# A four-layer graph network: layer 2's x turned by VectorE and ScalarE instead of TensorE, under a newly recorded order of steps

## The chip, the cores and the metric

The kernel runs on one core of one Trainium2 chip. The metric is device time in microseconds (us), the median over runs; smaller is better. A core has five engines with instruction queues of their own: TensorE (PE; its weight loads are shown apart as PEld), VectorE (DVE), ScalarE (ACT), GpSimd (POOL) and SyncE (SP), which here issues transfers. Engines wait for each other by semaphores. Within one queue the instructions stay in the order in which the program lists them.

## The reference, cut to what matters

Thirty-two graphs of 512 nodes with 256 features, fp32. Each goes through four layers, each with a residual and a layernorm:

```
x = layernorm(x + relu(((1 + eps) x + adj @ x) @ W1 + b1) @ W2 + b2)          # layer 0
x = layernorm(x + graph_attention(x, adj > 0.5; W, a_src, a_dst) + bias)      # layer 1, 4 heads
q, k, v = x @ Wq.T, x @ Wk.T, x @ Wv.T                                        # layer 2, 8 heads of 32
p = softmax(q k.T / sqrt(32) + log(adj + 1e-6))
x = layernorm(x + (p @ v) @ Wo.T + bo)
s = ((x @ W) @ x.T) * adj, masked by nodemask                                 # layer 3
x = layernorm(x + softmax(s) @ x)
```

## The kernel before, in words

**Steps.** `graph(g)` describes the work of one graph as named steps. A step has an engine, a cost in us, the steps that it comes after, the buffers that it takes and frees, and a function that emits its instructions. Transfers are steps of queues (`q1` for transfers issued by SP, `qa` for accumulating ones issued by POOL). `plan.run` puts the steps of all 32 graphs (and of the preparation, graph 0 of the plan) into one order, so that several graphs are in flight at once: while one is in layer 0, another is in layer 1, and so on. In the kernel before, `Plan.order` chooses at each point among the steps that can start soon the one that is due first; the due times come from a fixed period per graph, the length of the work left behind a step, and a long table of shifts, partly apart for the first and the last graphs (`edges`). The steps' costs serve this choice alone. The emitted order is the order in each engine's queue.

**Buffers.** SBUF tiles come from numbered stocks: 13 of kind B (8 KB per partition), 12 of kind C (4 KB), 10 of D (2 KB); PSUM has eight banks p.

**One graph.** x lies as a tile of 128 partitions x 4 chunks of nodes x 256 features, with nodes on the partitions.
- Layer 0: the adjacency is loaded by four transfers (`la0` to `la3`, line 821) and turned by VectorE (line 880); h0, h1 (hT_ps), f0 to f3 (h1T_ps), y0 and y1 (y_ps) are products on TensorE; then the residual (line 695), statistics (638, 639), one power on POOL (661), and the layernorm's four pieces on ScalarE (line 684, steps r10 to r13; r20 to r23 behind layer 1, r30 to r33 behind layer 2).
- Layer 1: x is turned on TensorE (line 978), v10 to v13, R_t (line 1035), the attention weights z on ScalarE (1104) and VectorE (1115), the products o_ps (1137), the denominators (1175), y_t (1204, 1205).
- Layer 2: x is needed with features on the partitions. `features_first(2)` turns it: two steps xt20, xt21, each with four 128x128 TensorE transposes into a PSUM bank (line 1241, xT_t), each followed by a ScalarE copy of 128x512 (line 1245, steps xe20, xe21). `proj` makes q and k (steps q0, q1, k0, k1, evicted by qe and ke, line 1264), `values` makes v (v20 to v23, evicted at line 1280). Eight scores steps s0 to s7 (line 1293) with four exps each on ScalarE (line 1306) and two multiplications by the adjacency on VectorE (line 1315), eight products n0 to n7 (line 1351). The weights are summed by accumulating POOL transfers (cd steps, line 1326; fd steps, line 1379), and d2 (line 1398) makes denominators of the sums. p0, p1 (o2p_ps) are the output projection.
- Layer 3: x (as x3) is turned by `turned`: one write to DRAM, four reads in a pattern, two VectorE transposes (line 742), save for the first two and the last three graphs, which use `features_first(3)`. Then iT (i0, i1), t0 to t3, exps (1545), w0 to w3.
- The bias of the next layer is added to x by an accumulating POOL transfer (`bias_steps`, line 625); for layer 2's bias it comes after the steps xt20, xt21.

`product` writes a matrix product in one of two forms: whole (line 342, array 128x128) or, if the step before left the array in 32-column tiles, as four 32-column pieces (line 346, array 128x32). Scores use an array of 32x128, d2 one of 64x32.

`moved`, which turns x in quadrants, stands in the kernel before, but nothing calls it.

Of the kernel before, what the change touches and what calls it, by code (L numbers as in the profile page):

```python
# [16 lines left out]
P = 128  # L17
# [19 lines left out]

class Step:
# [4 lines left out]
    def __init__(self, eng, us, after, take, mode, emit):  # L43
        self.eng, self.us, self.after, self.take, self.emit = eng, us, after, take, emit
        self.mode = mode
        self.then, self.frees = [], []


class Plan:
# [51 lines left out]
    def link(self):  # L101

        self.left = [{} for _ in self.steps]
        for g in reversed(range(len(self.steps))):
            steps, left = self.steps[g], self.left[g]
            for name, s in steps.items():
                for a in s.after:
                    (self.steps[0][a[1:]] if a[0] == "^" else steps[a]).then.append((g, name))
            for k, (_, after) in enumerate(self.frees[g]):
                for a in after:  # L110
                    steps[a].frees.append(k)
        for g in reversed(range(len(self.steps))):
            steps, left = self.steps[g], self.left[g]
            for name in reversed(steps):
                s = steps[name]
                left[name] = s.us + max(
                    (self.left[h][n] + self.hop(s, self.steps[h][n]) for h, n in s.then if h - g < 2),
                    default=0.0,
                )
# [6 lines left out]
    def ready(self, g, name, ends):  # L126

        s, t = self.steps[g][name], 0.0
        for a in s.after:
            h, n = (0, a[1:]) if a[0] == "^" else (g, a)  # L130
            t = max(t, ends[h][n] + self.hop(self.steps[h][n], s))
        return t

    def order(self, period, ahead, window, stay, rush=(), moves=(), edges=(0, (), 0, (), ())):


        room = {b: [(0.0, i) for i in range(n)] for b, n in self.stock.items()}
        engine, mode, out, last = {}, "", [], 0.0
        held = [{} for _ in self.steps]
        ends = [{} for _ in self.steps]  # L140
        waits = [{n: len(s.after) for n, s in steps.items()} for steps in self.steps]
        fwaits = [[len(after) for _, after in frees] for frees in self.frees]
        ready, low, opened = {}, 0, 0
        todo = [len(steps) for steps in self.steps]
        moved = dict.fromkeys((n for steps in self.steps for n in steps), 0.0)
        turn = [max(g - 1, 0) for g in range(len(self.steps))]
        for i, early in enumerate(rush):
            turn[-1 - i] -= early
        for n, far in moves:
# [1947 lines left out]
```

## Time and profile before

| | |
|---|---|
| median of 3 runs | 2767.73 us (2764.44 to 2769.32) |
| profiled execution, its own time | 2767.12 us |
| its span, first to last instruction | 2765.3 us |
| granted TensorE clock, mean | 0.994 |
| PE busy | 2716.7 us, 28680 matmul records |
| DVE busy | 2158.8 us, 4257 instructions |
| ACT busy | 1720.4 us, 3320 instructions |
| POOL busy | 474.8 us, 526 instructions |
| DMA queue of POOL's transfers / of SP's | 53.1% / 24.2% of 16 engines |

How to read it: the profile is one execution, recorded by the hardware. "Busy" is the time in which an engine ran at least one instruction; one matrix product in fp32 makes two matmul records, and records of neighbouring instructions overlap by about 0.1 us, so the pitch from start to start is shorter than the mean duration. A row such as "out<-in ... x508 | 273.9, 593 | 179.6 <-X" gives the shapes, the count, the busy time in us, the mean duration in ns, and the idle time of the engine just before such instructions with who ended most of it. In a timeline, merged rows give start, length, engine, line, tiles and count, with an idle time in brackets where there was one. Line numbers are those of the kernel before.

### The profile page before, as it was taken

The numbers are of one execution on the slowest core, as the hardware profiler recorded it, in microseconds if no ns is written. First come the engines' busy times: TensorE is split into PE (matmuls) and PEld (weight loads), VectorE is DVE, ScalarE is ACT, GpSimd is POOL, SyncE is SP. The second block draws the span as 40 slices with busy tenths as digits, with TensorE's granted clock in tenths as the row PEclk, the third lists the DMA queues.
The fourth block names the chain that finished last, engine by engine and source line by source line (L and its number), as shares of the span: only waits on it lengthen the run. The fifth ranks groups of instructions, "written<-read, shape, count | busy, mean of one in ns | idle before, by whom it ended". The sixth has DMA issues, their size and how long they took to land.

```text
span 2765.3 us, 68089 instructions
## 1 busy us (share of the span) xinstructions
PE 2716.7 (98%) x28680; PEld 1317.9 (48%) x28680; DVE 2158.8 (78%) x4257; ACT 1720.4 (62%) x3320; POOL 474.8 (17%) x526
## 2 busy tenths in 40 slices
PE   8999999999999999999999999999999999899998
PEld 6544444444445444445444445444444443444443
DVE  3887778877879877879877879877878877578975
ACT  3676665666666666666666666666665665556853
POOL 1111211121111121111121111121111111111110
PEclk9999999999999999999999999999999999999999
DMA  8487787778888879888878888888896988736760
GB/s 167 80 168 150 148 168 147 160 160 163 158 163 151 171 157 169 162 156 153 174 162 160 149 171 151 171 157 169 155 163 135 182 168 163 156 73 146 155 131 17
DMA packets 476735, 418.76 MB, mean 151 GB/s; under 512 B 377788, under 2 KB 431496, under 8 KB 444552
## 3 DMA queue, kind: packets, MB, share of 16 engines
q0 software_dynamic: 45568, 277.89, 53.1%
q1 hardware_dynamic: 429872, 136.18, 24.2%
q8 instruction: 227, 3.72, 0.5%
q14 instruction: 84, 0.69, 0.1%
q10 hardware_dynamic: 984, 0.28, 0.0%
HBM read 155.53 MB, written 31.24 MB: 68 GB/s over the span
## 4 chain that ended last, share of the span: by engine, by line
PE 86%; DVE 6%; DMA 3%; issue 2%; ACT 1%; POOL 0%; SPq 0%; DVEq 0%; POOLq 0%; ACTq 0%
PE s L1293 8%; PE o_ps L1351 7%; PE v_ps L346 7%; PE y_ps L342 7%; PE o_ps L346 6%; PE o_ps L1137 6%; PE hT_ps L346 6%; PE s L346 5%; PE h1T_ps L346 4%; PE o2p_ps L346 3%; PE iT_ps L342 3%; PE s L342 3%; PE h1T_ps L342 3%; PE kT_ps L342 2%; DVE z L1115 2%; PE qT_ps L346 2%
## 5 line engine op out<-in xcount | busy, mean ns | idle before, releaser
L1315 DVE SCALAR_TENSOR_TENSOR z<-AT,z 128x1024 f32<-128x1024 f32 x512 | 612.6, 1214 | 108.2 <-ACT z L1306 107.0
L1306 ACT ACTIVATE z<-s 128x512 f32<-128x512 f32 x1024 | 541.4, 608 | 109.2 <-PE s L1293 103.4
L1104 ACT ACTIVATE z<-R_bc,nT,S 128x512 f32<-128x512 f32 x512 | 373.4, 807 | 72.0 <-DMA z<-z 58.2
L684 ACT ACTIVATE x<-x,shift,rstd 128x256 f32<-128x256 f32 x508 | 273.9, 593 | 179.6 <-DVE shift L669 174.8
L1115 DVE SCALAR_TENSOR_TENSOR z<-z,T,edge 128x512 f32<-128x512 f32 x512 | 346.5, 742 | 5.8 <-ACT z L1104 5.8
L1326 POOL DMA_DIRECT2D z<-z x186 | 174.4, 942 | 868.4 <-PE o_ps L1351 445.3
L661 POOL TENSOR_TENSOR rstd<-ve,nhalf 128x4 f32<-128x4 f32 (+1 forms) x131 | 169.0, 1339 | 854.8 <-DVE ve L655 846.6
L1293 PE MATMUL s<-qT,kT 32*128 32x512 f32 x2048 | 278.4, 626 | 0.4 <-ACT kT L1264 0.4
L1351 PE MATMUL o_ps<-z,v 128*32 128x512 f32 x2048 | 254.9, 599 | 2.6 <-DVE z L1315 1.4
L1539 DVE TENSOR_TENSOR z<-s,AT 128x512 f32<-128x512 f32 x128 | 88.4, 690 | 214.9 <-PE s L342 110.1
L1137 PE MATMUL o_ps<-z,v 128*32 128x512 f32 x2048 | 233.8, 595 | 2.5 <-DVE z L1115 2.5
L1165 DVE TENSOR_TENSOR z<-z 128x1024 f32<-128x1024 f32 (+1 forms) x256 | 229.5, 949 | 0.7 <-PE o_ps L1137 0.7
L638 DVE BATCH_NORM_STATS2 st<-x 128x6 f32<-128x256 f32 x508 | 212.7, 419 | 10.6
L346 PE MATMUL o_ps<-x,z 128*32 128x257 f32 x3520 | 202.4, 380 | 0.0
L346 PE MATMUL hT_ps<-AT,x 128*32 128x256 f32 (+2 forms) x2640 | 185.5, 380 | 0.0
L342 PE MATMUL y_ps<-w_sb,h1T 128*128 128x256 f32 x832 | 184.4, 379 | 0.0
L342 PEld LDWEIGHTS y_ps<-w_sb,h1T 128*128 128x128 f32 x832 | 156.1, 190 | 21.5 <-issue 1.0
L1293 PEld LDWEIGHTS s<-qT,kT 32*128 32x128 f32 x2048 | 96.7, 184 | 143.5 <-issue 63.6
L346 PEld LDWEIGHTS o_ps<-x,z 128*32 128x32 f32 x3520 | 114.8, 110 | 83.8 <-issue 6.9
L346 PE MATMUL h1T_ps<-hT,w_sb 128*32 128x512 f32 x1296 | 147.9, 595 | 0.0
L625 POOL DMA_DIRECT2D x<-biases x96 | 103.8, 1081 | 237.0 <-issue 67.7
L346 PE MATMUL s<-iT,xT 128*32 128x512 f32 x1232 | 139.4, 592 | 0.1
(188 smaller groups left out, 3858.7 us busy)
## 6 DMA issues: line engine op xcount, KB each, us to landing
z<-z POOLq DMA_DIRECT2D x186, 1024.0 KB, 8.7
x<-biases POOLq DMA_DIRECT2D x96, 512.0 KB, 9.6
R_bc<-R_dram SPq DMA_DIRECT2D x32, 1024.0 KB
Ar<-in_adj_dram SPq DMA_DIRECT2D x124, 256.0 KB
z<-z POOLq DMA_DIRECT2D x62, 512.0 KB, 7.7
x<-in_x_dram SPq DMA_DIRECT2D x32, 512.0 KB
out_dram<-x SPq DMA_DIRECT2D x31, 512.0 KB
x_dram<-x SPq DMA_DIRECT2D x27, 512.0 KB
```

The source lines that it names most:

```text
L342: nc.tensor.matmul(out, lhsT, rhs, start=start, stop=stop)
L346: nc.tensor.matmul(out[part], lhsT[:, part], rhs, start=start, stop=stop)
L638: nc.vector.bn_stats(t[f"st{n}"][:, c, :], t["xo" if n == 4 else "x"][:, c, :D])
L684: nc.scalar.activation(t[into][:, c, :D] if into else xn, xn, AF.Identity, bias=t[f"shift{n}"][:, c : c + 1], scale=t[f"rstd{n}"][:, c : c ...
L1104: nc.scalar.activation(t[f"e{h}"][:, c, :], t["Rbc"][:, h, :], AF.Relu, bias=t["nT"][:, h, c : c + 1], scale=t["S"][:, h, c : c + 1],)
L1115: nc.vector.scalar_tensor_tensor(z, z, t["T"][:, h, c : c + 1], t["edge"][:, c, :], op0=ALU.add, op1=ALU.mult)
L1137: nc.tensor.matmul(po[32 * q : 32 * q + 32, :], t["v"][:, c, hp * P + 32 * q : hp * P + 32 * q + 32], t[f"e{2*hp+q//2}"][:, c, :], start=( ...
L1165: nc.vector.tensor_add(z[:, :m, :], z[:, :m, :], z[:, m : 2 * m, :])
L1293: nc.tensor.matmul(pk, t["k"][hs, o, blk(c)], t["q"][hs, o, :], start=True, stop=True)
L1306: nc.scalar.activation(t[f"E{k}"][:, j, :], t[f"ps{k}{j}"], AF.Exp, scale=QSCALE)
L1315: nc.vector.scalar_tensor_tensor(z, t["AT"][:, c, None, :].to_broadcast([P, 2, N]), ADJ_EPS, z, op0=ALU.add, op1=ALU.mult,)
L1351: nc.tensor.matmul(t[f"n{o}"][32 * j : 32 * j + 32, :], t["v2"][:, c, o * P + F2 * j : o * P + F2 * (j + 1)], t[f"E{k}"][:, j, :], start=( ...
```

## The change

Graphs that are `near` an end (the first two and the last three) keep `features_first(2)`. The other 27 call `moved(2, ("L2",), "x", True)`: two VectorE transposes of 128x512 (steps xu20, xu21) turn each 32x32 block in place within its group of 32 partitions, into one more C buffer xU2, and sixteen ScalarE copies (four steps xe20 to xe23 of four copies) move each group's blocks to the right group of partitions. Each copy has 32 partitions and 256 elements, in runs of 32. q, k and v wait for all four steps. The bias transfer of layer 2 comes after xu20, xu21. The planned cost of such a copy step is set higher.

The search inside `Plan.order` is gone. `ORDER`, a compressed text, holds the order of all steps; `sequence` unpacks it, and `run` follows it, keeping only the books on buffers and on the array's shape. The order was found with the planner's costs, its two ends in a search of their own in which transfers stand in order of issue. It differs from the old one in every part, the middle too.

```diff
+ORDER = (
+    'c-rk;*_PwF4FmyhT5P$OxqWjd{r|riRDqP;bMl<LNZqz&i3?CzNFA1$(mW)I;A6ZAPv)V1h{k2S`xpPFqmF8{pty-!xZnlMkL3T7'
...
+)
...
-    def order(self, period, ahead, window, stay, rush=(), moves=(), edges=(0, (), 0, (), ())):
...
+    def sequence(self, text):
+        data = zlib.decompress(base64.b85decode(text))
+        left, low = [list(steps) for steps in self.steps], 0
+        for ahead, place in zip(data[: len(data) // 2], data[len(data) // 2 :]):
+            g = low + ahead
+            yield g, left[g].pop(place)
+            while low < len(left) and not left[low]:
+                low += 1
...
+        for g, name in self.sequence(text):
...
+            s.emit()
...
+        XE2 = DC if near else 4
...
-                    f"xe{n}{b}", "act" if shared else "dve", 1.35 if shared else 1.6,
+                    f"xe{n}{b}", "act" if shared else "dve", 1.66 if shared else 1.6,
...
-        features_first(2, ("L2",))
-        bias_steps(3, row("xt2", DC))
+        if near:
+            features_first(2, ("L2",))
+            bias_steps(3, row("xt2", DC))
+        else:
+            moved(2, ("L2",), "x", True)
+            bias_steps(3, row("xu2", DC))
...
-                f"{n}{o}", "pe", 1.72, row("xe2", DC) + prev(n, o) + (f"^we{n}",),
+                f"{n}{o}", "pe", 1.72, row("xe2", XE2) + prev(n, o) + (f"^we{n}",),
...
-                f"v2{c}", "pe", 0.86, row("xe2", DC) + prev("v2", c) + ("^wev",),
+                f"v2{c}", "pe", 0.86, row("xe2", XE2) + prev("v2", c) + ("^wev",),
...
+        plan.run(ORDER)
```

The body of `moved` for this call (it is unchanged, and not called before):

```
for d in range(DC):                      # steps xu2d, VectorE
    nc.vector.transpose(xU[:, d, :] as (p c f), x[:, :, blk(d)])
for b in range(4):                       # steps xe2b, ScalarE
    for a in range(4):
        nc.scalar.copy(xT[32b:32b+32] at [j, d, c, a, i], xU[32a:32a+32] at [j, d, c, b, i])
```

## The prediction

> **What bounds the kernel now.** I read the page's busy shares first, then busy time by stretches of the span, then one graph's TensorE timeline, then the waits of TensorE and the rows by shape.
>
> From the page, busy time by engine and TensorE's share in 40 slices:
> ```profile
> PE 2716.7 (98%) x28680; PEld 1317.9 (48%) x28680; DVE 2158.8 (78%) x4257; ACT 1720.4 (62%) x3320; POOL 474.8 (17%) x526
> ...
> PE   8999999999999999999999999999999999899998
> ```
> Busy time by stretches (length, then PE, PEld, DVE, ACT, POOL, clock, DMA):
> ```profile
> 600.00:900.00 300.00, 300.00 (x3335) 146.80 (x3331) 247.91 (x494) 189.72 (x362) 54.18 (x57) 1.00 0.84 158
> ...
> 2100.00:2400.00 300.00, 286.06 (x3129) 130.37 (x3122) 213.55 (x422) 170.58 (x329) 51.49 (x57) 0.98 0.83 162
> ...
> 2700.00:2766.00 66.00, 52.30 (x466) 24.69 (x458) 33.60 (x86) 22.94 (x41) 5.68 (x9) 0.92 0.05 18
> ```
> In the middle TensorE has no idle time, while ScalarE idles 37% and VectorE 17% of it. All 48.6 us of TensorE's idle time (2765.3 less 2716.7) is at the two ends: 16 us up to 600 and 33 us after 2100, by the same view.
>
> One graph's turn in the middle, in TensorE's timeline (start, length, work):
> ```profile
> 1002.27 0.28 PE L1035 MATMUL R_t<-ident,R 128*18 128x128 f32 x1
> ...
> 1054.92 3.60 PE L342 MATMUL iT_ps<-xT,w_sb 128*128 128x512 f32 x8
> 1058.35 1.04 PE L1241 MATMUL xT_t<-ident,x 128*128 128x128 f32 x8
> 1059.32 1.92 PE L1351 MATMUL o_ps<-z,v 128*32 128x512 f32 x16
> ...
> 1085.24 0.28 PE L1035 MATMUL R_t<-ident,R 128*18 128x128 f32 x1
> ```
> R_t comes once per graph, so a graph costs 82.97 us. Nothing between the two rows has an idle mark: the period is TensorE's work. The eight xT_t transposes of layer 2 hold TensorE from 1058.35 to 1059.32.
>
> A page of the Trainium skill speaks against this reading: Perfetto Trace Analysis, Identifying the Most-Contended Engine, calls matmul busy time a poor measure and goes by weight loads. By that rule (PEld 48%) VectorE at 78% would be the engine to spare, and this change, which loads it more, would bring no gain. The rows of start times decide: one matmul follows the other at a fixed pitch.
>
> **The change part by part.**
>
> *Transposes off TensorE, 27 graphs.* Of the 0.97 us above, 0.10 is the price of the next row's other array shape (one 128-column transpose follows another at 0.109 us in the timeline; the last is 0.2 before the o_ps). So 8 x 0.109 = 0.87 us, times 27 = **23.5 us off the bounding engine**. This is on the path, since no other engine fills those stretches.
>
> *Array shapes.* Each change of tiling (128x128, 128x32, 32x128, 64x32) costs TensorE 0.09 to 0.11 us: 128x512 matmuls start 0.43 apart inside a shape and 0.52 across a border. The instruction order of the two programs has 541 borders before and 474 after. Borders out of the 32x128 scores are free, for the next scores step starts 0.51 later as well; without them 354 become 303. 51 x 0.105 = **5.4 us less**, nearly all at the ends (the middle has 17 paying borders per graph in both). Many y_ps and h1T_ps products change between 128x128 and 128x32; that is free, as eight 256-column records take 1.73 us in either (x32 rows of 7.06 and of 1.93 per quarter).
>
> *Added on VectorE.* Two 128x512 transposes per graph. The nearest rows are the adjacency's and layer 3's; on ScalarE, the copies' neighbours are these (busy, mean ns, idle before):
> ```profile
> L684 ACT ACTIVATE x<-x,shift,rstd 128x256 f32<-128x256 f32 x508 | 273.9, 593 | 179.6 <-DVE shift L669 174.8 <-DVE rd_all L1565 4.7
> ...
> L1545 ACT ACTIVATE z<-z,node_off 128x512 f32<-128x512 f32 x128 | 89.8, 718 | 50.8 <-DVE z L1539 50.8
> ...
> L938 ACT ACTIVATE h1T<-h1T_ps,b_sb 128x512 f32<-128x512 f32 x128 | 87.9, 687 | 81.0 <-PE h1T_ps L346 51.8 <-PE h1T_ps L342 29.0
> ...
> L880 DVE STREAM_TRANSPOSE AT<-Ar 128x512 f32<-128x512 f32 x124 | 77.7, 678 | 0.0
> ...
> L1245 ACT COPY xT<-xT_t 128x512 f32<-128x512 f32 x74 | 42.6, 591 | 69.2 <-PE xT_t L1241 69.2
> ...
> L1280 ACT COPY v<-v_ps 128x256 f32<-128x256 f32 x128 | 41.5, 385 | 22.8 <-PE v_ps L346 17.6 <-PE v_ps L342 4.9
> ```
> 2 x 0.69 x 27 = 37 us more, 2196 of about 2730, 80%. It lies beside TensorE's work.
>
> *Added on ScalarE.* Sixteen copies of 32 partitions x 256 elements, SBUF to SBUF, from one group of 32 partitions to another. No row has that. Low end: L1280, the same element count out of PSUM, whose four take 1.20 us in the timeline, 0.27 each as they overlap. High end: a 128x512 activation from SBUF (L1104) at 807 ns, about 0.71 per piece back to back. In between lies L684 (SBUF, 256 elements, with scale and bias) at 593, four in 2.08 us, 0.49 each. SBUF instead of PSUM costs 31 ns (L1545 against L938), so a bare copy is 385 + 31 = 416 ns; I take **0.42 us** a piece, with no overlap counted, as the four-part pattern is not in the trace. 16 x 0.42 = 6.7 us; two evictions of about 0.48 go. Net 5.7 x 27 = 154 us: ScalarE at 1874, 69%.
>
> The other rule to weigh: the Trainium skill's VectorE: DVE Perf Modes, Rules for kernel authors, gives 128x128 transposes to TensorE where the result may land in PSUM. By it each graph would trade 0.87 + 1.0 us for 1.4 + 6.7 and lose 6 us, 167 in all. The stretch of 600 to 900 answers that this is true of work, but not of time: there ScalarE has 110 us idle in 300 and TensorE none.
>
> *Does the longer chain stay hidden?* q, k and v2 now wait for four copy steps. In the new order, from the end of scores step s7 TensorE does n4, y0, y1, i0, n5, n6, i1, n7 and then k0 of the waiting graph: 0.96 + 6.94 + 1.73 + 1.74 + 1.73 + 0.87 = 14.0 us by the pitches. ScalarE in that time: three exps at 0.48, four layernorm pieces at 0.49, three exps: 4.9, so free at 5.0; VectorE's two transposes (0.60 back to back) run from the last layernorm piece at 3.6 to 4.9. Copies from 5.0 to 11.8. **2.1 us to spare**; up to 0.55 us a copy is hidden. Behind the copies on ScalarE stand the evictions of i1 and i0, due later (i1 ends at 13.1). The x tile's bias DMA on POOL (L625, landing in 9.6) now waits for VectorE's transposes instead of TensorE's, and is needed by x30 more than 50 us later: nothing. The turned tile holds one more of the twelve C buffers from the transposes to the last copy, about 8 us of each turn; a later tile's first write could wait for it, which I leave within the new waits below.
>
> *The ends.* One wait there is large (TensorE timeline):
> ```profile
> 2375.25 3.74 PE L346 MATMUL v_ps<-wg_sb,xT 128*32 128x264 f32 x64
> 2386.96 3.41 PE L346 MATMUL iT_ps<-xT,w_sb 128*32 128x512 f32 x16 [7.96 <-DVE xT L742]
> ```
> iT waits 7.96 us for layer 3's x on its way through DRAM, and then runs at half pace (3.41 for sixteen records that else take 1.9): 9.5 us lost. Counted in the orders, the TensorE work between the last layernorm piece r33 and i0 of such graphs grows from 18 to 19 us to 21 to 28. I take 8 us won here. The remaining starts (4.47 us until the first adjacency, 3.3 more in the next rows) and the serial last graph stand in both orders. Bounds for the ends: all 33 us of tail idleness won, or 20 us of new waits, as one new 8 us wait like this at each end costs.
>
> Sum, against the profiled execution (2767.1 us, span 2765.3, so 1.8 around it): 2767.1 - 23.5 - 5.4 - 8.0 = 2730.2. New waits in the middle I put at 0.1 us a graph, 3 us: **2733**. The median of the runs shown, 2767.73, is 0.6 above the profiled one, within rounding of this.
>
> **The rivals.**
> *Transfers take over the middle.* The sum of the denominators d2 comes after a chain of three accumulating DMAs; in the middle the last lands only 0.4 to 3.2 us before d2 starts, and layer 3's x lands 0 to 3.4 us before its transposes. The new order leaves 24.4 us of TensorE work from n7 to d2 instead of 26.0, and 18.2 instead of 19.1 from r33 to i0. If the chains take as long as now, up to 1.2 us a graph is waited: 27 x 1.2 = 32; half of that on average gives about 2749, all of it 2762. Against: n6 to d2 is unchanged (26.9), and n6 is what the chain waits for. Chance 0.22.
> *The copies come late* (the slower side). Place: k0 waits for the sixteenth copy. The gain of 37 us is gone when the wait is 1.4 us a graph, that is at 3.5 us over the 6.7, or 0.64 a copy. At L1104's 0.71, 11.3 us, the wait is 2.5 us: 2733 + 27 x 2.5 = 2800. For: the pattern is in no row. Against: 256 elements, not 512, and no scale or bias. With other orders' mishaps, chance 0.10.
> *The change doesn't do what it says*: TensorE's saved time reappears as idle time before the same waits, the period stays 82.97. About 2765. Chance 0.04.
> *The ends gain more*: 20 us or so of the tail's idleness; 2712. Chance 0.12.
>
> **How the numbers follow.** The forecast, 2720 to 2745, has 0.52, and its time is the predicted one. The range of 2705 to 2763 takes in the better ends and the transfers' case, and leaves out about 0.05 below and 0.13 above. About 0.2% (5.5 us) is what a measurement of this kernel can tell from no change. Faster: 0.52 + 0.22 + 0.12 = 0.86; same 0.04; slower 0.10.
>
> **What would show it.** Right: R_t to R_t at about 82.1 us in the middle, with TensorE at 300 of 300; xT_t rows of L1241's kind down from 296 to 80; ScalarE near 69%, each copy near 0.42 us; no 8 us wait before iT. Wrong: an idle mark at kT_ps released by ScalarE's copy (the second rival), at d_ps or iT_ps released by a DMA or VectorE (the first), or a tail with more than 33 us idle.

## The result, and the profile after

The changed kernel takes **2796.52 us** (median of 4 runs, 2791.48 to 2805.82) against 2767.28 for the kernel before (4 runs): 1.0115 times as long, 95% interval 1.0098 to 1.0133. It is slower by 29 us where the forecast was faster by 35. The profiled execution took 2792.94 us, with a span of 2791.2.

The busy shares and TensorE's 40 slices, as they were read before:
```profile
PE 2706.1 (97%) x30576; PEld 1297.3 (46%) x30576; DVE 2185.6 (78%) x4311; ACT 1854.5 (66%) x3698; POOL 469.1 (17%) x526
...
PE   9999999999999999999999999999999999989998
```
TensorE has less work than before (2706.1 against 2716.7 us), and more idle time: 85.1 us instead of 48.6. The slices cannot show it, since a 9 stands for 90% and more. The first of the stretches shown before does (length, then PE, PEld, DVE, ACT, POOL, granted clock, DMA share, GB/s):
```profile
600.00:900.00 300.00, 284.92 (x3367) 137.57 (x3363) 234.63 (x468) 194.27 (x390) 50.32 (x55) 0.98 0.77 150
```
From 600 to 900 TensorE was busy all 300 us before; now it lacks 15 us there, and its granted clock is 0.98 instead of 1.00. The waits name the place (us in total, times, longest):
```profile
DVE xT L721 <- DMA xL<-x_dram: 62.1, 11, 10.2
...
PE iT_ps L324 <- DVE xT L721: 47.8, 10, 7.3
```
Before, the second kind of row had one wait, of 8.0 us. Now iT, layer 3's first product, waits ten times for VectorE's transposes of layer 3's x, and these wait for the reads of that x from DRAM. One wait is near the end (7.3 us), one is of 0.3 us, and eight are in the middle, 4.5 to 5.4 us each, 40.3 in all.

Two graphs of the changed kernel side by side, in TensorE's timeline (start, length, work, the idle time before it in brackets). The first one is late, the second is not:
```profile
1054.19 7.09 PE L324 MATMUL y_ps<-w_sb,h1T 128*32 128x256 f32 x128
1066.23 3.64 PE L324 MATMUL iT_ps<-xT,w_sb 128*32 128x512 f32 x16 [4.95 <-DVE xT L721]
1069.61 3.05 PE L1339 MATMUL o_ps<-z,v 128*32 128x512 f32 x16
...
1144.57 7.09 PE L324 MATMUL y_ps<-w_sb,h1T 128*32 128x256 f32 x128
1151.51 1.92 PE L324 MATMUL iT_ps<-xT,w_sb 128*32 128x512 f32 x16
1153.23 1.93 PE L1339 MATMUL o_ps<-z,v 128*32 128x512 f32 x16
```
The late graph pays twice: it waits 4.95 us, and then sixteen records take 3.38 us from start to start instead of 1.72. The granted clock (column before the last two) tells why. The two stretches lie behind the late and the timely iT:
```profile
1066.00:1071.00 5.00, 4.77 (x24) 1.35 (x28) 4.90 (x10) 0.00 (x0) 0.00 (x0) 0.50 1.29 142
...
1151.00:1156.00 5.00, 5.00 (x58) 1.86 (x52) 4.90 (x10) 4.86 (x13) 0.47 (x1) 1.00 0.83 150
```
In every trace here this clock changes only on a fixed grid, whose slots are 3.41 us long. Four slots around the late iT, in the same columns:
```profile
1061.65:1065.07 3.42, 0.00 (x0) 0.00 (x0) 0.00 (x0) 3.32 (x10) 0.00 (x0) 1.00 1.09 146
1065.07:1068.48 3.41, 2.25 (x12) 0.68 (x16) 3.11 (x4) 0.73 (x2) 0.00 (x0) 0.50 1.17 135
1068.48:1071.90 3.42, 3.42 (x20) 0.89 (x16) 3.25 (x10) 0.00 (x0) 0.00 (x0) 0.50 1.09 111
1071.90:1075.31 3.41, 3.41 (x36) 1.07 (x32) 0.98 (x6) 0.87 (x2) 1.92 (x2) 1.00 0.39 78
```
The slot in which TensorE did nothing is followed by half the clock, and the first slot that it worked through is followed by the full clock. In the eight late graphs the half clock lasts one slot (three times) or two (five times).

By the starts of R_t a timely turn takes 82.4 us and the eight late ones 88.9 to 90.7: together 59.6 us over 82.4, or 7.45 a late graph, of which 5.0 is the wait and 2.4 the slow matmuls behind it.

The span in three stretches, by the fifth and the twenty-fifth R_t:

| kernel | before the 5th R_t | 20 turns | after the 25th R_t | span |
|---|---|---|---|---|
| before | 335.8 | 1662.1 | 767.4 | 2765.3 |
| changed | 321.7 | 1694.4 | 775.1 | 2791.2 |
| x3, the changed kernel with the reads on time | 320.5 | 1649.8 | 759.3 | 2729.6 |

### The profile page after: what moved, and what is told of

Same layout as the page of the kernel before. It is cut to its first block, busy times and chain, and to the rows that moved or that the text cites. A ratio compares the mean times of both kernels' runs of the same rounds, so it can differ in the third digit from the quotient of the medians.

```text
span 2791.2 us, 72411 instructions
## 1 busy us (share of the span) xinstructions
PE 2706.1 (97%) x30576; PEld 1297.3 (46%) x30576; DVE 2185.6 (78%) x4311; ACT 1854.5 (66%) x3698; POOL 469.1 (17%) x526
## 4 chain that ended last, share of the span: by engine, by line
PE 68%; DVE 16%; DMA 8%; issue 2%; SPq 2%; ACT 2%; POOL 1%; ACTq 0%; POOLq 0%; DVEq 0%
PE s L1281 7%; DVE z L1094 6%; PE o_ps L1339 6%; PE v_ps L324 5%; PE s L324 5%; PE h1T_ps L320 5%; PE iT_ps L324 4%; PE y_ps L324 4%; DMA xL<-x_dram 4%; PE o_ps L1116 4%; DVE z L1144 3%; PE o_ps L324 3%; PE hT_ps L324 3%; PE s L320 2%; DMA x_dram<-x 2%; DVE z L1303 2%
## 5 line engine op out<-in xcount | busy, mean ns | idle before, releaser
L1303 DVE SCALAR_TENSOR_TENSOR z<-AT,z 128x1024 f32<-128x1024 f32 x512 | 604.4, 1209 | 51.8 <-ACT z L1294 51.4
L1314 POOL DMA_DIRECT2D z<-z x186 | 172.3, 929 | 979.4 <-PE o_ps L1339 348.8
L324 PE MATMUL o_ps<-x,z 128*32 128x257 f32 x3680 | 210.8, 380 | 0.0
L324 PE MATMUL hT_ps<-AT,x 128*32 128x256 f32 (+2 forms) x2736 | 193.5, 382 | 0.5 <-issue 0.4
L320 PE MATMUL h1T_ps<-hT,w_sb 128*128 128x512 f32 x424 | 191.0, 592 | 0.0
L324 PE MATMUL y_ps<-w_sb,h1T 128*32 128x256 f32 x3392 | 188.7, 379 | 0.0
L761 ACT COPY xT<-xU 32x256 f32<-32x256 f32 x432 | 173.9, 402 | 12.0 <-DVE xU L742 6.3
L917 ACT ACTIVATE h1T<-h1T_ps,b_sb 128x512 f32<-128x512 f32 x128 | 86.6, 687 | 143.2 <-PE h1T_ps L320 128.7
L324 PE MATMUL iT_ps<-xT,w_sb 128*32 128x512 f32 x992 | 131.6, 658 | 47.8 <-DVE xT L721 47.8
L324 PEld LDWEIGHTS o_ps<-x,z 128*32 128x32 f32 x3680 | 136.0, 110 | 79.4 <-issue 14.9
L324 PE MATMUL s<-iT,xT 128*32 128x512 f32 x1472 | 165.9, 592 | 0.0
```

What stands on the lines that cost most here:

```text
L320: nc.tensor.matmul(out, lhsT, rhs, start=start, stop=stop)
L324: nc.tensor.matmul(out[part], lhsT[:, part], rhs, start=start, stop=stop)
L1303: nc.vector.scalar_tensor_tensor(z, t["AT"][:, c, None, :].to_broadcast([P, 2, N]), ADJ_EPS, z, op0=ALU.add, op1=ALU.mult,)
```

## The experiments

Theory: in the new order a 1 MB adding transfer of GpSimd (step cd5, L1314) is issued at the same time as the last of the four reads of layer 3's x. A read that comes to the DMA engines behind it lands only with it. Rival 1: the new work of VectorE or ScalarE is late, not the reads. Rival 2: there are too many bytes for the stretch, in whatever order.

The queues in the late graph (start, length, queue, work), GpSimd's first, then SyncE's:
```profile
1038.39 1.20 POOL L1314 DMA_DIRECT2D z<-z  x1
1050.15 0.82 POOL L1367 DMA_DIRECT2D z<-z  x1 [10.56 <-DMA z<-z]
...
1055.46 0.94 POOL L1314 DMA_DIRECT2D z<-z  x1
```
```profile
1040.10 0.57 SPq L689 DMA_DIRECT2D x_dram<-x  x1
1051.05 5.25 SPq L702 DMA_DIRECT2D xL<-x_dram  x4
1056.46 12.05 SPq L800 DMA_DIRECT2D Ar<-in_adj_dram  x4
```
The write of x goes out at 1040.10, 1.7 us behind a first adding transfer (cd2), and has landed only when that one has, 10 us later (L1367, which waits for cd2, follows at 1050.15). So the reads start at 1051.05; the last is issued at 1055.6, just behind cd5 at 1055.46. It lands at 1065.2, and cd5 at 1064.7. Over the middle graphs of this kernel, counted from the write: cd5 is always issued at +15.3 or +15.4; last reads issued up to +14.9 land at about +18 to +20, in time for iT at +21; those issued at +15.2 and later land at +25; at +15.0 both occur. (The issue of a read takes 0.6 us or more on SyncE's queue; by its end the border is sharp: in time up to +15.70, late from +15.71.)

Why a read lands with the adding transfer is in the packets of the two queues, which the trace counts, each with its size (packets, MB, share of 16 engines; q0 is GpSimd's queue, q1 SyncE's). First the 3 us from 1059 of the late graph, while cd5 is on its way, then the 1 us from 1064, when its packets are through:
```profile
DMA packets 146, 0.61 MB, mean 202 GB/s; under 512 B 73, under 2 KB 73, under 8 KB 73
q0 software_dynamic: 73, 0.60, 103.1%
q1 hardware_dynamic: 73, 0.01, 4.1%
```
```profile
q1 hardware_dynamic: 1214, 0.15, 147.1%
```
The read consists of 1024 packets of 128 bytes, cd5 of 128 packets of 8 KB. While both queues have work, the packets go one for one: 73 to 73 here, 24 of SyncE's in a microsecond instead of 1214. So what is left of a read when cd5's packets start (1.5 to 2.6 us behind its issue) is still mostly there when they end. In the midst of cd5, 87 of its packets went with 32 to 145 of SyncE's in the twenty middle graphs, median 85.5. The write of x, packets of 1 KB, is held by cd2 in the same way (92 to 95 from 1043 to 1047).

| run | us (median) | against before, 95% |
|---|---|---|
| x1 add later | 2733.81 | 0.9885 (0.9869 to 0.9902) |
| x2 load before read | 2898.68 | 1.0484 (1.0462 to 1.0507) |
| x3 write first | 2730.48 | 0.9872 (0.9855 to 0.9888) |
| x4 turns doubled, on x1 | 2759.76 | 0.9982 (0.9973 to 0.9992) |
| x5 sums first, on x3 | 2735.76 | 0.9885 (0.9857 to 0.9913) |
| x6 both moves of x1 and x2 | 2788.41 | 1.0081 (1.0054 to 1.0108) |
| x7 half the copies doubled, on x3 | 2808.34 | 1.0153 (1.0131 to 1.0175) |
| x8 turn in the planner's own new order | 3645.29 | 1.3179 (1.3153 to 1.3205) |
| x9 order alone | 2882.24 | 1.0427 (1.0409 to 1.0444) |
| x10 order alone, write first | 2877.66 | 1.0417 (1.0395 to 1.0439) |
| x11 three edits on the changed kernel | 2727.95 | 0.9866 (0.9850 to 0.9883) |
| x12 turn alone in the old order | 2937.44 | 1.0621 (1.0599 to 1.0642) |
| x13 add in two, on x2 | 2876.54 | 1.0403 (1.0373 to 1.0433) |
| x14 add in four, on x2 | 2869.48 | 1.0378 (1.0348 to 1.0408) |
| x15 add behind the reads, on x2 | 2755.83 | 0.9977 (0.9947 to 1.0006) |

The edits move steps in the fixed order: `run` makes a list of what `sequence` yields, changes it, and follows it. The expectations below count nine late graphs in the middle; one of these was the wait of 0.3 us, so it is eight.

### x1: the second adding transfer later
```diff
+        for g in range(4, 27):
+            order.remove((g, "n4"))
+            order.insert(order.index((g + 2, "y0")) + 1, (g, "n4"))
```


> The changed kernel, with one step moved in its fixed order: the product of z and v of one head (step n4, o_ps at L1339, 8 matmuls, 1.06 us) goes behind the first half of the next graph's y_ps product (3.5 us of TensorE), which delays the 1 MB adding transfer behind it (L1314, cd5) by about 3 us. Theory (order of issue): in 9 of the 22 middle graphs of the changed kernel the last of the four reads of layer 3's x (L702) was issued beside or behind that transfer, 15.0 to 15.6 us after the write, and landed only with it, at +25; iT then waited 5 us and ran slowly behind, 7.5 us a graph. With the transfer issued at about +18 every read goes first: no iT wait in the middle, turns of 82.4 us, 2796 - 9 x 7.5 = 2729 us (2720 to 2740). Rival 1 (the vector transposes and scalar copies of the new turn are late, not the reads): nothing of them is moved, 2796 us. Rival 2 (the transfers are too many bytes for the stretch whatever their order): the wait moves to the d2 product, which the later transfer feeds, 2785 to 2800 us.

Measured: 2733.81 us. In the middle cd5 goes out at +18.3 to +18.9, and last reads issued as late as +16.1 land at +20.8 or sooner. The waits (us in total, times, longest):
```profile
PE iT_ps L328 <- DVE xT L725: 5.9, 5, 4.2
```
4.2 of the 5.9 us is the wait near the end; the middle has 1.7. No work of VectorE or ScalarE was moved, so rival 1 falls; no byte was taken away, and d2 does not wait, so rival 2 falls.

### x2: the last read later
```diff
+        for g in range(5, 26):
+            order.remove((g + 4, "la0i"))
+            order.insert(order.index((g, "xl33i")), (g + 4, "la0i"))
```


> The changed kernel, with the issue of one load of a later graph's adjacency (la0, Ar at L800) moved ahead of the last of the four reads of layer 3's x on the same issuing engine, in 21 middle graphs: the last read is issued some 0.7 to 1.2 us later, nothing else is moved. Theory (order of issue): nearly all those reads are now issued behind the 1 MB adding transfer that goes out at +15.3 and land with it, so that 18 to 21 graphs wait in place of 9: 9 to 12 more x 7.5 = 2864 to 2886 us. Rival 1 (vector and scalar work late): the same time, 2796 us. Rival 2 (bytes, not order): the bytes are the same, within 1 us a graph, 2796 to 2810 us.

Measured: 2898.68 us, a little over the expected range. All 21 graphs wait:
```profile
PE iT_ps L328 <- DVE xT L725: 127.4, 21, 12.1
```
One of the 21 is the long wait near the end; a wait of 4.6 us of the middle is put down to a ScalarE copy and stands in another row. By graph, the 21 of the middle wait 119.8 us, 5.7 each, and their turns are 89 to 92 us. The bytes are the same as in the changed kernel. But this load also puts its own 256 KB ahead of the read; x6 and x15 take that apart.

### x3: the write first
```diff
+                if k == 2 and 5 <= g <= 25:
+                    nc.gpsimd.tensor_copy(little([P, 1], "hold2"), graphs[g - 1]["x3"][:, 3, :1])
                 nc.gpsimd.dma_start(dst, src, accum_op=ALU.add)
```


> The changed kernel, with a copy of 128 x 1 elements on GpSimd ahead of the first 1 MB adding transfer (L1314, cd2), which reads the last quarter of layer 3's x: the transfer is so issued just behind the write of that x to DRAM (L689) in place of 1.7 us ahead of it. Theory (order of issue): the write then lands some 4 to 5 us after its issue and not at +8 to +10 with the transfer, the reads go out at +5 to +9 and land before the second transfer is issued at +15.3; no iT wait, 2796 - 68 = 2729 us (2720 to 2745), if the later first transfer does not make the d2 product late (it landed 1.8 to 6.3 us ahead of it). Rival 1: 2796 us. Rival 2: the d2 product waits in place of iT, 2780 to 2800 us.

Measured: 2730.48 us. GpSimd's queue, then SyncE's, in one middle graph:
```profile
1018.31 0.47 POOL L1315 COPY hold<-x 128x1 f32<-128x1 f32 x1 [1.44 <-ACT x L664]
1018.84 0.87 POOL L1317 DMA_DIRECT2D z<-z  x1
```
```profile
1018.20 0.57 SPq L690 DMA_DIRECT2D x_dram<-x  x1
1024.54 5.27 SPq L703 DMA_DIRECT2D xL<-x_dram  x4
```
With the adding transfer 0.6 us behind the write instead of 1.7 us ahead, the reads start 6.3 us after the write, where the late graph had 10.9, and all are issued 4 to 6 us ahead of cd5. iT does not wait in the middle at all.

The trace of before had shown this rule already, in rows that the prediction did not read. SyncE's and GpSimd's queues for two graphs of the kernel before (L710 is the write, L723 the reads, L1326 the adding transfer):
```profile
1862.50 0.57 SPq L710 DMA_DIRECT2D x_dram<-x  x1
1866.60 12.42 SPq L723 DMA_DIRECT2D xL<-x_dram  x4
```
```profile
1864.68 1.22 POOL L1326 DMA_DIRECT2D z<-z  x1
```
```profile
1943.88 0.57 SPq L710 DMA_DIRECT2D x_dram<-x  x1
1957.96 2.76 SPq L723 DMA_DIRECT2D xL<-x_dram  x4
```
```profile
1943.68 1.22 POOL L1326 DMA_DIRECT2D z<-z  x1
```
(In both a smaller adding transfer, L1379, goes out 0.5 us ahead of the one shown.) An adding transfer 2.2 us behind the write lets the reads start 4.1 us after it; one that is 0.2 us ahead of it holds them back to 14.1 us.

### x4: TensorE's transposes put back elsewhere
```diff
+                if not near:
+                    nc.tensor.transpose(pt[:, 0, :], t["yT"][:, 0, blk(c)], ident)
+                    nc.tensor.transpose(pt[:, 1, :], t["yT"][:, 1, blk(c)], ident)
```


> The kernel of the run that issues the second adding transfer later, with the 8 TensorE transposes of layer 1's y (L1183, L1184) done twice in each of the 27 inner graphs: the work that the change took from TensorE is put back on it at a place where nothing else is altered. If TensorE sets the pace once the waits are gone, the time rises by the price of the prediction, 27 x 8 x 0.109 = 23.5 us over that run (21 to 27): about 2753 us. Rival (TensorE is not the bound behind the change, transfers or VectorE are, so that the removal of the transposes was worth little): less than 8 us over that run.

Measured: 2759.76 us, 26.0 over x1 by the medians, 22.4 by the spans of the profiled executions. The better measure is a turn in which nothing waits: 83.3 us against 82.4, 0.9 for the 0.87 that the prediction put. So TensorE's work sets the pace, and eight transposes are worth what the prediction said. That the totals come near 23.5 us too is partly luck: of the 22.4 us the 20 middle turns gave 15.0 (some turns of x1 hold short waits), and 10 came behind the 25th R_t, where the wait for iT grew from 4.2 to 11.9 us.

### x5 and x11: the last tenths of a turn
x5 moves VectorE's last two sums for d_ps (as01, as21) ahead of the row sums of hs (hsl), and the first transposes of y behind f0:
```diff
+        for g in range(6, 28):
+            for name in ("as01", "as21"):
+                order.remove((g, name))
+                order.insert(order.index((g, "hsl")), (g, name))
+            order.remove((g, "yt0"))
+            order.insert(order.index((g + 1, "f0")) + 1, (g, "yt0"))
```


> The kernel of the run that writes layer 3's x first, with two more steps moved in 22 graphs: VectorE adds the last two pairs of layer 1's z (L1145, 2 x 0.65 us, what the d_ps product waits for) ahead of the two row sums of hs (L1057, 0.87 us) in place of behind them, and TensorE does the first of the h1T products (1.72 us) between d_ps and the first transposes of y, which cover the later hs. Theory: the 0.5 us by which a turn of the middle is still longer than predicted (82.4 against 82.1 with 1.57 us in place of 1.08 us for the 32 matmuls of d_ps) is a wait of d_ps for those sums, since they end 0.4 us behind its first records; turns of 82.0 us, 22 x 0.4 = 9 us less than that run, about 2721 us. Rival (the 0.5 us is the pace of TensorE behind the 257-column products): turns of 82.4 us, 2730 us. If hs becomes late for the transposes instead: 2730 to 2745 us.

Measured: 2735.76 us (2728.39 to 2742.82), turns of 82.3. In one graph of x3 d_ps started at 1102.40, and VectorE ended its sums (L1145) at 1102.86. With the sums first, the time of TensorE from the starts of d_ps records to the next starts fell from 2.44 to 1.95 us a turn. The wait was real; but s rose by 0.31 us and h1T by 0.14. The gain was given back to what came next. That the median is 5 us above x3's comes from the end: in the profiled executions the 20 turns are 2.8 us shorter, but the wait for iT near the end is 12.7 us instead of 7.3.

x11 is x3 with the sums first but yt0 left in place, and with R_bc's load and cd5 behind the reads in the 28th graph, where x3 still waited 7.3 us:
```diff
+        order.remove((30, "Rli"))
+        order.insert(order.index((28, "xl33i")) + 1, (30, "Rli"))
...
+                if k == 5 and g == 28:
+                    nc.gpsimd.tensor_copy(little([P, 1], "hold2"), graphs[g - 1]["xL3"][:, 0, :1])
```


> The changed kernel with three edits: the write of layer 3's x issued ahead of the first adding transfer; VectorE's last two sums for d_ps ahead of the row sums of hs in 22 graphs, this time without moving the first transposes of y; and near the end (the 28th graph of 32) the 1 MB load of R_bc and the second adding transfer issued behind the four reads of layer 3's x, which landed 7.3 us late there. Theory: 2730.5 - 22 x 0.4 - 7 = 2715 us (2706 to 2724), turns of 82.0 us, no wait of iT above 1 us anywhere. Rival (the wait of 0.4 us moves on to the product of s or to the transposes of y, as in the run with the moved transposes): turns of 82.3 us, 2720 to 2730 us. If the held transfers make the d2 product of the 29th graph late: 2725 to 2735 us.

Measured: 2727.95 us, the fastest median of the study (0.9866 of before), though not told apart from x3 by its interval, and outside the theory's 2706 to 2724. The wait near the end is gone, and that turn fell from 82.0 to 78.7 us. In the middle the rival was right: 82.3, d_ps down 0.33 us a turn, the transposes of y and s up 0.26.

### x6, x15, x13, x14: what does the read wait for?
x6 has the moves of x1 and x2 together, both diffs unaltered.

> The changed kernel with two of the moves together: the load of the adjacency ahead of the last read (2898.7 us alone) and the second adding transfer 3 us later (2733.8 us alone). It tells whether the late reads of the first were late behind the load's own bytes or behind the 1 MB adding transfer. Theory (the adding transfer): the reads are issued at +16 again, but nothing of 1 MB is issued ahead of them; they land at +20 to +22 and iT waits 0 to 1 us; 2735 to 2755 us. Rival (the load's bytes): the waits of 5 to 6 us stay, 2870 to 2900 us.

Measured: 2788.41 us, between the theories:
```profile
PE iT_ps L331 <- DVE xT L728: 52.4, 16, 6.9
```
Six graphs wait 6.4 to 6.9 us, nine 0.2 to 1.7. In the six the read lands at +26.6 to +27.0, again with cd5 (+26.0 to +26.3), though in five of them its issue began 2.1 to 2.7 us ahead of cd5's. But behind the load these issues took 3.2 to 3.4 us. SyncE's row and GpSimd's in one of the five:
```profile
706.83 3.15 SPq L709 DMA_DIRECT2D xL<-x_dram  x1
```
```profile
709.33 0.93 POOL L1321 DMA_DIRECT2D z<-z  x1 [2.91 <-ACT z L1301]
```
The read's issue ended at 709.98, 0.65 us behind the start of cd5's. By the end of the issue the rule of the changed kernel holds here too, in all 21 graphs: reads issued in full by +18.8 land by +21.8, those from +18.9 on at +26.6 and later, with cd5 at +18.3 in all but four. So the load delays the read's issue, and the adding transfer does the rest.

x15 is x2 with cd5 held until the reads have landed:
```diff
+                if k == 5 and 5 <= g <= 25:
+                    nc.gpsimd.tensor_copy(little([P, 1], "hold5"), graphs[g - 1]["xL3"][:, 0, :1])
```


> The same kernel (adjacency load ahead of the last read) with the second adding transfer whole, but held on GpSimd by a copy of 128 x 1 elements that reads what the four reads bring, so that it is issued only when they have landed. It tells what the load's own bytes cost the read once no adding transfer can stand ahead of it. Under both theories: the reads land at +19 to +22 after the write, iT waits 0 to 1 us, 2735 to 2755 us. If the bytes of the load were the cause of the 5.7 us: 2870 us or more.

Measured: 2755.83 us, at the end of the expected range. The median wait of the 21 graphs is 1.0 us instead of 5.7, 20.4 us in all instead of 119.8. So the load alone costs a graph 1 us, the adding transfer the other 4.7.

x13 and x14 are x2 with cd5 in two and in four parts:
```diff
-                nc.gpsimd.dma_start(dst, src, accum_op=ALU.add)
+                w = 4 * N // (2 if k == 5 else 1)        # x14: 4
+                for i in range(0, 4 * N, w):
+                    nc.gpsimd.dma_start(dst[:, i : i + w], src[:, i : i + w], accum_op=ALU.add)
```


> The kernel of the run with an adjacency load ahead of the last read (21 graphs wait 5.7 us each for iT, 2898.7 us), with the second 1 MB adding transfer issued as two transfers of half the columns (4 KB of each partition), one right behind the other. Theory A (a read that comes to the DMA engines behind an adding transfer waits for that whole transfer, and may go between two): the read lands with the first half, some 4 us sooner; iT waits 1 to 2 us a graph or none: 2740 to 2780 us. Theory B (it is the order of issue alone, or the bytes ahead of the read: nothing goes between): the waits stay at 5 to 7 us, 2890 to 2910 us.

> The same with the second adding transfer in four transfers of a quarter of the columns. Theory A: the read lands with the first or second quarter, no wait of more than 1 us, 2735 to 2760 us, unless the three more issues on GpSimd make a later product wait. Theory B: 2890 to 2915 us.

Measured: 2876.54 and 2869.48 us; the median wait is 5.7 us in both, as with one piece. But the reads fall in two groups. In four graphs the issue of the read ended by +16.5 (x13) or +16.7 (x14); in x2 these graphs waited 4.6 to 5.5 us, here 1.7 to 2.1 and 0.6 to 0.7. (A fifth gained in each, where parts of cd5 went out later.) In the others the issue, held up behind the load, ended between +17 and +24.4, and the read landed with the last part or behind it. Between the parts SyncE's queue does get through, as in this microsecond of x13:
```profile
q1 hardware_dynamic: 1129, 0.14, 93.6%
q0 software_dynamic: 21, 0.02, 13.8%
```
So theory A holds for a read that stands early enough in its queue to use the gap. For the others theory B's times came out; that the gap went to the load ahead of them is likely, but not shown. The parts make 256 packets of 4 KB in x13 and 512 of 2 KB in x14, still fewer than the read's 1024. In x14 SyncE's queue at times got far less than one for one (20 packets against 230 in 2 us of one graph); why is open. The changed kernel itself, without the load in front, was not run with a cut transfer.

### x7: the price of a copy
x3 with the copies of odd a done twice:
```diff
+                            for _ in range(1 + a % 2):
                                 nc.scalar.copy(
```


> The kernel of the run that writes layer 3's x first, with 8 of the 16 ScalarE copies of the turn (L761) done twice: 8 x 0.40 = 3.2 us more in each of the 27 inner graphs, as if one copy took 0.60 us. The copies of that run end 1.28 us ahead of k0's first product in the middle (median). Theory (the prediction's rival with its threshold): k0 waits 3.2 - 1.3 = 1.9 us a graph, 27 x 1.9 = 52 us, 2782 us (2770 to 2795). If other work of ScalarE behind the copies becomes late as well: above 2795. If ScalarE had more to spare than the 1.28 us: below 2760.

Measured: 2808.34 us, 78 over x3 where 52 were expected. The waits of k and q for the copies are as expected, 52.4 us. But of the 21 graphs in the middle eight run slowly behind a wait of 2 us (sixteen records in 2.9 to 3.4 us, not 1.74), their turns are 86.2 to 86.6 us instead of 84.7 to 85.0, and the wait for iT near the end grew to 12.4. In the 20 middle turns 57 us were lost against x3, for 41 us of waits.

Which of the waits bring the half clock is set by the grid of 3.41 us. Two slots of a slow graph, then two of a fast one, each with a wait of 2.06 or 2.05 us:
```profile
731.19:734.61 3.42, 1.36 (x16) 0.27 (x12) 0.53 (x4) 3.25 (x9) 2.04 (x2) 1.00 1.06 195
734.61:738.02 3.41, 3.41 (x20) 0.87 (x16) 0.00 (x0) 3.38 (x8) 0.00 (x0) 0.50 1.00 187
...
560.53:563.94 3.41, 2.31 (x24) 0.50 (x16) 1.51 (x7) 3.26 (x9) 2.30 (x3) 1.00 0.72 127
563.94:567.35 3.41, 2.46 (x24) 0.81 (x28) 0.16 (x1) 3.31 (x8) 0.61 (x1) 1.00 1.13 229
```
In the slow one the whole wait lies in one slot (2.06 us idle), in the fast one it is divided (1.10 and 0.95). So in all 21: in the eight slow graphs a slot has 1.97 us idle or more, in the other thirteen none has over 1.8.

### x8, x12, x9, x10: one part of the change alone
x8 puts the turn into the kernel before and lets its planner order the steps.
```diff
-        features_first(2, ("L2",))
-        bias_steps(3, row("xt2", DC))
+        if near:
+            features_first(2, ("L2",))
+            bias_steps(3, row("xt2", DC))
+        else:
+            moved(2, ("L2",), "x", True)
+            bias_steps(3, row("xu2", DC))
```

> The kernel before, with its own planner and its own order of transfers, and only the turn of layer 2's x replaced by the quadrant transposes and the 16 copies in the inner graphs. In the order that the planner then finds, the second adding transfer goes out right behind the write of layer 3's x and nothing of 1 MB between its reads and their use, but the first product that needs the copies (k0) stands right behind the 7 us of y_ps and 1 us of s, while the chain to it (statistics and rescaling 3 us, transposes 1.4 us, copies 6.6 us) takes 11 us. Theory (transfers of the changed kernel lost its gain, the turn itself is sound): no wait of iT for a DMA; the time is 2767 - 29 = 2738 us plus 2 to 4 us a graph that k0 waits for the copies, 2790 to 2845 us, and all of the new waits are at kT_ps. Rival (the turn itself makes the reads late, whatever the order): iT waits for xL here too, in 8 graphs or more.

Measured: 3645.29 us, far from every number. TensorE's largest waits, and the longest for the reads:
```profile
PE kT_ps L346 <- ACT xT L782: 218.4, 22, 10.7
PE d_ps L1175 <- DVE z L1165: 104.3, 23, 10.0
...
PE iT_ps L346 <- DVE xT L742: 7.9, 1, 7.9
```
Two waits of TensorE are for the reads, this one and one of 5.5 us, both behind the middle. The new waits are at many places, and a turn takes 118 to 121 us. That the planner's long list of offsets fits no other set of steps is likely, but not shown. The run says nothing of the turn's price.

x12 says more: the old order is kept in the middle, step by step; the transposes' steps issue VectorE's two, and the second eviction's step issues the 16 copies.
```diff
-                        nc.tensor.transpose(pt[:, blk(c)], t[src][:, c, blk(d)], ident)
+                nc.vector.transpose(
+                    t["xU2"][:, d, :].rearrange("p (c f) -> p c f", c=NC), t["x"][:, :, blk(d)]
+                )
...
-                    nc.scalar.copy(t[f"xT{n}"][:, d, :], t[f"pt{d}"])
+                for b in range(4 if d else 0):
+                    for a in range(4):
+                        nc.scalar.copy(
...
```

> The kernel before with the order that it had in the middle, and only the turn exchanged: in the place of TensorE's 8 transposes VectorE does the two quadrant transposes, and ScalarE does the 16 copies in the place of its second eviction. Theory (the turn needs the new order for its 8 us chain, and the new order brings the late reads): k0 stands 2 us behind the old transposes, so it waits 5 to 7 us for the copies in each of the 27 inner graphs, while TensorE is spared 0.97 us; no wait of iT for the reads; 2767 + 27 x (4 to 6) = 2875 to 2930 us. Rival (the chain is covered in the old order too, the new order was not needed): 2735 to 2770 us.

Measured: 2937.44 us. k0 waits 3.3 us a graph, less than expected, yet a turn takes 88.5 us (83.0 before): much of the rest is slow matmuls behind the wait (granted clock 0.66 to 0.67 in the 5 us behind most of these) and a further wait of o_ps, 0.5 us a graph:
```profile
PE kT_ps L346 <- ACT xT L1267: 66.1, 21, 3.3
```
x9 has the new order with TensorE's transposes at the place of VectorE's (their steps emit the 8 transposes, two of the four copy steps the evictions); x10 is the same with the write first.
```diff
-            moved(2, ("L2",), "x", True)
+                @step(f"xu2{d}", "pe", 0.437, row("r2", NC) + prev("xu2", d), take=(f"p=xt2{d}",))
...
+                        nc.tensor.transpose(pt[:, blk(c)], t["x"][:, c, blk(d)], ident)
...
+                    if b < DC:
+                        nc.scalar.copy(t["xT2"][:, b, :], t[f"pt{b}"])
```

> The changed kernel's fixed order, with layer 2's x turned by TensorE again in the 27 inner graphs: the step that had the two quadrant transposes on VectorE does the 8 TensorE transposes into two PSUM banks, the first two of the four ScalarE steps evict them, the others do nothing. So the new order alone, without the turn. Theory (the new order of issue makes the loss, the turn is sound): the adding transfers and the reads stand as in the changed kernel, iT waits 5 us in 5 to 12 graphs again, and TensorE has 0.87 us a graph more to do: 2796 + 23.5 = 2820 us (2800 to 2840). Rival (the VectorE and ScalarE part of the turn makes the reads late): no waits of iT, 2740 to 2770 us.

> The same kernel with TensorE's transposes back, with the write of layer 3's x issued ahead of the first adding transfer as in the run that did this to the changed kernel (2730.5 us). Beside that run it prices the turn in one and the same order with no late read in either. Theory: 27 x 0.87 = 23.5 us more, and up to 27 x 0.2 for borders of array shape that the transposes add: 2754 to 2760 us, no wait of iT in the middle. Rival (the turn's gain on TensorE is eaten by later vector and scalar work even without late reads): within 10 us of 2730.

Measured: 2882.24 and 2877.66 us; neither theory had this. In that place the rescaled x is not ready, and TensorE waits for it, in order, in front of the y_ps products:
```profile
PE xT_t L1239 <- ACT x L663: 58.9, 88, 5.2
```
A turn takes 88.5 us, iT comes 6 us later and finds its reads landed, so the two runs hardly differ. They don't price the turn in one order; x4 prices the transposes alone. With x12 they show that the new turn in the old order and the old turn in the new order both lose, as they were placed here.

## Why the prediction was wrong, step by step

**The step that failed** is in the first rival: "If the chains take as long as now, up to 1.2 us a graph is waited". It named the mechanism's place (the reads of layer 3's x) and gave it 0.22, but took the landing for a quantity that moves by tenths of a microsecond as the TensorE work ahead of it does. The runs show a step: a read that meets an adding transfer lands 5 to 6 us later, since it gets one packet of 128 bytes for each of the transfer's 8 KB, and any other lands in time. That rival was to cost 32 us at most; the changed kernel pays 59.6 for eight graphs and x2 172 over x3 (2901.8 against 2729.6 by span) for 21. It was also seen only as a lag of TensorE work between r33 and i0. What had moved was the queue of GpSimd against that of SyncE: a 1 MB transfer, which in the middle of the kernel before was never issued between the reads and iT, now stands at +15.3. The same step is missing from the sum, where "New waits in the middle I put at 0.1 us a graph, 3 us" stands for what measured 59.6 us.

**Every wait was priced at its length.** The price is 7.45 for a wait of 5.0 in the changed kernel, 8.1 for 5.7 in x2, and 57 us for 41 in the 20 middle turns of x7. The prediction had the row for it (3.41 instead of 1.9 behind the 7.96 us wait) and used it for the ends alone. The granted clock of 0.50 behind the wait, above, is the cause. TensorE: Matmul & The Clock Gate of the Trainium skill, Part 1, gives the same halving: half rate after an idle window of about 3.4 us, full rate after a busy one of the same length, the windows running on by themselves. The ratio agrees, and so does the window: the slots of 3.41 us above, and half clocks of one or two slots in the eight late graphs. What differs is the condition: in x7 a window with 2 us idle was enough.

**Transposes, 23.5 us:** right. L1241's rows are gone from the inner graphs (80 records are left of 296), and x4 measures 0.9 us a turn for the 0.87.

**Array shapes, 5.4 us, nearly all at the ends:** not measured apart. In the middle the time of v_ps up to the next starts rose from 7.15 to 7.49 us a turn and that of hT_ps from 6.93 to 7.09; borders moved there, other groups lost as much.

**The period, 82.1:** 82.4 in timely turns. 0.41 us of d_ps more, a wait for VectorE's sums (x5), is as large as what is missing, though x5 and x11 removed most of it and won only 0.1; the prediction had put 0.1.

**VectorE and ScalarE:** right. 2185.6 us against 2196, 1854.5 against 1874, and the copy, estimated at 0.42 us between far bounds, took 402 ns:
```profile
L761 ACT COPY xT<-xU 32x256 f32<-32x256 f32 x432 | 173.9, 402 | 12.0 <-DVE xU L742 6.3 <-DVE shift L648 0.9
```
**The longer chain, 2.1 us to spare:** hidden, as forecast; x3 has 1.28 us to spare (median of the middle). The second rival did not occur, but its price was too low, as x7 shows.

**The ends, 8 us:** in x3 the two outer stretches of the table give 23.4 us (15.3 and 8.1). Of the prediction's terms 6.1 for the transposes of seven graphs, 5.4 for borders, 8 and less 0.7 for waits belong there, 18.8. The 20 turns gave 12.3 where 17.4 less 2 were forecast. The 8.0 us wait that was to go came back a graph later with 7.3 us. x11 took it away, by putting a load of SyncE's queue and an adding transfer behind the reads; which of the two it was is not shown. The forecast of 2733 us is what x1 (2733.8) and x3 (2730.5) reach, by terms that are partly off in opposite directions; that they agree this closely is luck.

**The rule on VectorE transposes,** weighed in the prediction, is answered by x3, x4 and x12: the exchange pays here while idle time covers 8 us of chain, and loses 170 us where it does not.

**How the two queues are served.** DMA: Bandwidth & Descriptors of the Trainium skill, Queues, rings and completion order, says that an engine takes turns between queues, one packet of some 9 to 17 descriptors at a time. The turns are in the trace, 73 packets to 73 in the late graph and 80 to 80 in 3 us of x2. A bundle of 9 to 17 of one queue's does not show in these counts.

## What to carry to other kernels

Where a short transfer sits on the critical path, list every queue in the order of issue, across engines, and look for a large transfer that has moved in front of it or beside it: the loss comes as a whole transfer's time or not at all, so an average per turn hides it. Compare the sizes of the two transfers' packets too: where packets go one for one, the queue with the small ones stands almost still. The trace before usually has both cases, early and late, in different turns; compare these first. And price a wait of TensorE with the slow matmuls behind it: here half as much again as its length.

## What the runs showed of the hardware that was not expected

- Two queues with work shared the DMA engines about packet for packet, although one's packets are 64 times as large: 73 of 128 bytes to 73 of 8 KB (changed kernel). A 128 KB read that meets a 1 MB adding transfer therefore lands with it, 5 to 6 us late. What counts is the end of the read's issue, which behind a 256 KB load came 3 us after its start (x6).
- The granted clock changes on a grid of 3.41 us. In x7 a slot of it with 1.97 us idle or more was followed by the half clock, and one with up to 1.8 us was not, so that equal waits of 2 us cost differently by where they fall. In the middle turns of the changed kernel and of x6 waits of 4.5 us and more were always followed by it, waits up to 1.7 us never.
- The issue of a read on SyncE's queue can itself be held up: 3.2 to 3.4 us behind a load in x6, and in x2, with an adding transfer running as well, a single one took 7.68 us,
```profile
1081.76 7.68 SPq L706 DMA_DIRECT2D xL<-x_dram  x1
```
  against 0.6 to 2.5 us each in a graph of x3, so that everything behind it on the queue was late as well.
